# Graph attention on one core: the column of ones written by GpSimd, three one-hots cast together one tile ahead, a third buffer for the turned one-hots

## The chip, the core and the metric

The program runs on one core of a Trainium2 chip. The core has a matrix engine (TensorE, "PE" in the profile, its weight loads "PEld"), a vector engine (VectorE, "DVE"), a scalar engine (ScalarE, "ACT"), a general engine (GpSimd, "POOL", which also issues the indirect DMAs of this kernel) and a DMA-issuing engine (SyncE, "SP"). The metric is the device time of one execution in microseconds. Before the change it is 3703.74 us, the median of 9 runs from 3694.52 to 3710.56 us.

## What is computed

A graph of 3,125 nodes with 256 features and 53,125 edges sorted by destination goes through eight layers, each added to its input: graph attention, a small mixture of experts, three rounds of graph convolution, a routed mixture of experts, and so on. The change lies in the first layer, the attention:

```python
q = (nfeat @ Wq.T).reshape(n, HEADS, HEAD_DIM) / SCALING
k = (nfeat @ Wk.T).reshape(n, HEADS, HEAD_DIM)
v = (nfeat @ Wv.T).reshape(n, HEADS, HEAD_DIM)
attn = jnp.einsum('ehd,ehd->eh', k[src], q[dst]) + attn_bias
a = jnp.exp(attn - m[dst])                    # m: maximum over a node's edges
a = a / segment_sum(a, dst)[dst]
out = segment_sum(v[src] * a[:, :, None], dst).reshape(n, FEAT) @ Wo.T
```

There are 8 heads of 32 features each. For each edge the key and value rows of its source are needed, and the query of its destination; what the edges give is summed by destination.

## The kernel before

**Tiles.** The 3,125 destinations are 25 tiles of 125 (`T`, `P`). Since the edges are sorted by destination, a tile's edges are one window of 18 chunks of 128 edges (`WC`), handled as three parts of 6 chunks (`PC`). Keys and values of all nodes are computed in the beginning and written to `kv_d` in HBM, one row of 512 numbers per node.

**A tile's data.** Each part has a tile `kv` of [128 edges, 6 chunks, 528 columns] float32 (line 1652, seven buffers, so two tiles and a part). Columns 16 to 527 hold the gathered key and value rows, one indirect DMA for each chunk (line 1661), 18 for a destination tile. Column 15 (`KO - 1`) holds ones, so that the sum over the edges also counts them; VectorE writes it after the six gathers are issued (line 1667). Columns 7 to 14 later take the weights of the 8 heads.

`oh` (line 1821, two buffers, bf16) is the one-hot of an edge's destination within the tile, an edge per partition, made by VectorE (line 282, called from `one_hot`). `oht` (line 1811, two buffers, bf16) is the same turned, a destination per partition: SyncE loads the edges' destinations, spread over the partitions (issued by `move`, lines 107 and 108), and VectorE compares them in place (line 1839). `oh_f` (line 1893, two buffers) is a part of `oh` cast to float32 by ScalarE (line 1894).

**The steps of a tile t.** `asked` issues the loads. `one_hot`, `one_hot_turned` and `queries` (lines 1820 to 1840) make the two one-hots and the query in three bf16 pieces (`q_t`). `logits` (line 1842), once for each part, multiplies `oht` by the pieces (TensorE, line 1851, results `qx` in two PSUM buffers), multiplies the keys by that in place (VectorE, line 1854) and sums by head (line 1855). `sums_of` adds the bias (line 1861), takes a scaled exponential (ScalarE, line 1864), sums it by destination (TensorE, line 1867) and copies the sums (ScalarE, line 1869). `weights_of` makes a shift from these (line 1875), brings it to the edges (TensorE, line 1879), subtracts it (lines 1880 and 1882) and takes the exponential into `kv` (ScalarE, line 1884). `weighted` (line 1886) multiplies the values by the weights (VectorE, line 1889, in place), casts the one-hot and accumulates 18 chunks in `acc` (TensorE, line 1896, 36 matmul records a tile). When a part's matmuls have read its `kv` buffer, that buffer is free, and the next six gathers into it can start. `normed`, `normed_turned` and `projected` divide, transpose and project the result and add it to `x`.

**The order of the work.** The loop at line 1927 works on three tiles at once: loads for t + 1, logits and sums of t ("now"), weights and accumulation of t - 1 ("before"), one-hots and queries of t + 1 ("after"):

```python
if now: logits(now, 0)
beside()
if before: weights_of(before); beside(); weighted(before)
beside()
if after: one_hot(after)
if before: normed(before)
if after: one_hot_turned(after); queries(after)
...
if now: logits(now, 1)        # then normed_turned, logits(now, 2), projected, sums_of
```

`beside` is a step of the next layer's experts (`Experts0`, line 793) for pairs of finished tiles, and from tile 5 on there are steps of `Windows` (line 1988). They share all engines with the attention. This is not the order of issue: when the program is built, each engine's instructions are put into one fixed sequence, the earlier in the text the sooner, but an instruction that is planned to be ready may pass one that is not. In the trace the query product of line 1828 for tile t + 1 (at 542.3 us) stands ahead of the accumulation of tile t - 1 (548.9 us), though the text has it behind. On the chip an engine then keeps to its sequence and waits wherever an instruction isn't ready. The time at which a buffer comes free is part of that plan.

On GpSimd a gather also waits until the one five before it has landed (`under_way`, lines 1664 and 1665).

Of the kernel before, what the change touches and what calls it, by code (L numbers as in the profile page):

```python
# [10 lines left out]
F32 = mybir.dt.float32  # L11
F32R = mybir.dt.float32r
I32 = mybir.dt.int32
BF16 = mybir.dt.bfloat16
# [9 lines left out]
P, T = 125, 25  # L24
# [24 lines left out]
WC, PC = 18, 6  # L49
# [21 lines left out]
def gnn_ffn_kernel(ctx: ExitStack, tc: tile.TileContext, a, out: bass.AP):  # L71
    nc = tc.nc
# [32 lines left out]
    def move(queue, to, of):  # L105

        queue.dma_start(to[:SPREAD], of[:SPREAD])
        return queue.dma_start(to[SPREAD:], of[SPREAD:])
# [1518 lines left out]
    def attention(windows, experts):  # L1627
# [9 lines left out]
        KO, VO, AO = 16, 16 + D, 7  # L1637
        WB = T * WC // 5
        with ExitStack() as es:
# [11 lines left out]
            def rows_tile():  # L1651
                return tiles.tile([128, PC, 2 * D + KO], F32, name="kv", bufs=7)
# [3 lines left out]
            def gathered(at):  # L1656


                kv = rows_tile()
                for c in range(PC):  # L1660
                    got = nc.gpsimd.indirect_dma_start(  # L1661
                        out=kv[:, c, KO:], out_offset=None, in_=kv_d,
                        in_offset=bass.IndirectOffsetOnAxis(ap=src_i[:, at + c:at + c + 1], axis=0))
                    if len(under_way) > 4:
                        tc.add_manual_dep(got.ins, under_way[-5].ins.name, data_dep, reason="in turn")
                    under_way.append(got)
                nc.vector.memset(kv[:, :, KO - 1:KO], 1.0)
                return kv


# [1 line left out]
            pool = setup.enter_context(tc.tile_pool(name="att_in", bufs=2, reuse_waits="tile"))  # L1672
# [107 lines left out]
            for i, (t0, n) in enumerate(GROUPS):  # L1780
                both = rows_tile().rearrange("p c w -> p (c w)")
                ln = both[:P, :4 * D].rearrange("p (i d) -> p i d", i=4)
                kv = both[:P, 4 * D:12 * D].rearrange("p (i d) -> p i d", i=4)
# [17 lines left out]
            pool = es.enter_context(tc.tile_pool(name="att_s", bufs=2, reuse_waits="tile"))  # L1801
# [6 lines left out]
            def asked(t):  # L1808
                s = Tile()
                s.t, s.kv = t, begun if t == 0 else []  # L1810
                s.oht = pool.tile([P, WC, 128], BF16, name="oht")
                move(nc.sync, s.oht.rearrange("d c e -> d (c e)"), turned_d[t * WC:(t + 1) * WC, :].rearrange("(o c) e -> o (c e)", o=1)
                     .to_broadcast([P, WC * 128]))
                s.lt = pool.tile([128, 2, P], F32, name="lt_t")
                nc.sync.dma_start(s.lt, lt_d[:, :, t, :].rearrange("k f p -> f k p"))
                s.eb = pool.tile([128, H, WC], F32, name="eb_t")
                nc.sync.dma_start(s.eb, eb_d[:, t])
                return s

            def one_hot(s):  # L1820
                oh = pool.tile([128, WC, HC], BF16, name="oh")
                one_hots(oh, row_h[:, s.t * WC:(s.t + 1) * WC, :], iota_h)
                s.oh = oh[:, :, :P]
# [13 lines left out]
            def one_hot_turned(s):  # L1837
                v = s.oht.rearrange("d c e -> d (c e)")
                nc.vector.tensor_scalar(v, v, pcol[:P], None, ALU.is_equal)
                s.l = pool.tile([128, WC, H], F32, name="l")  # L1840

            def logits(s, p):

                if p == len(s.kv):
                    s.kv.append(gathered(s.t * WC + p * PC))
                kv = s.kv[p]
                for c0 in range(0, PC, 2):
                    ps = psum.tile([128, 2, D], F32, name="qx", bufs=2)
                    for c in range(2):
                        for k in range(3):  # L1850
                            nc.tensor.matmul(ps[:, c, :], s.oht[:, p * PC + c0 + c, :], s.q[:, k, :],  # L1851
                                             start=(k == 0), stop=(k == 2))
                    k_ = kv[:, c0:c0 + 2, KO:VO]
                    nc.vector.tensor_mul(k_, k_, ps)  # L1854
                nc.vector.tensor_reduce(  # L1855
                    s.l[:, p * PC:(p + 1) * PC, :],
                    kv[:, :, KO:VO].rearrange("p c (h d) -> p c h d", h=H), AX.X, ALU.add)
# [13 lines left out]
            def weights_of(s):  # L1871

                m = pool.tile([P, H], BF16, name="m")
                c = 8.0 * math.log(2.0)
                nc.vector.tensor_scalar(m, sums[:, s.t, :].bitcast(I32), c / 2.0 ** 23, -127.0 * c,
                                        ALU.mult, ALU.add)
                ps = psum.tile([128, WC, H], F32, name="sm")
                for c in range(WC):
                    nc.tensor.matmul(ps[:, c, :], s.oht[:, c, :], m, start=True, stop=True)
                nc.vector.tensor_sub(s.l, s.l, ps)  # L1880

                nc.vector.tensor_scalar(s.l, s.l, 20.0, None, ALU.min)
                for p in range(WC // PC):
                    nc.scalar.activation(s.kv[p][:, :, AO:AO + H], s.l[:, p * PC:(p + 1) * PC, :], AF.Exp)

            def weighted(s):
                s.acc = psum.tile([P, 512], F32, name="acc", bufs=1)
                for p, kv in enumerate(s.kv):
                    nc.vector.tensor_mul(  # L1889
                        kv[:, :, KO:VO].rearrange("p c (h d) -> p c h d", h=H),  # L1890
                        kv[:, :, VO:].rearrange("p c (h d) -> p c h d", h=H),
                        kv[:, :, AO:AO + H].unsqueeze(3).to_broadcast([128, PC, H, HD]))
                    of = pool.tile([128, PC, P], F32, name="oh_f")
                    nc.scalar.copy(of, s.oh[:, p * PC:(p + 1) * PC, :])
                    for c in range(PC):
                        nc.tensor.matmul(s.acc[:, :D + H + 1], of[:, c, :], kv[:, c, AO:VO],  # L1896
                                         start=(p == 0 and c == 0), stop=(p == 2 and c == PC - 1))


            def normed(s):  # L1900
                nc.scalar.copy(deg[:, s.t:s.t + 1], s.acc[:, H:H + 1])
                inv = pool.tile([P, H], F32, name="inv")
                nc.vector.tensor_scalar(inv, s.acc[:, 0:H], 1.0e-30, None, ALU.max)
                nc.vector.reciprocal(inv, inv)
                s.ao = pool.tile([P, D], F32, name="ao", bufs=1)
                nc.vector.tensor_mul(s.ao.rearrange("p (h d) -> p h d", h=H),
                                     s.acc[:, H + 1:D + H + 1].rearrange("p (h d) -> p h d", h=H),
                                     inv.unsqueeze(2).to_broadcast([P, H, HD]))

            def normed_turned(s):  # L1910
                ps = psum.tile([128, 2, P], F32, name="sm")
                for k in range(2):
                    nc.tensor.transpose(ps[:, k, :], s.ao[:, k * 128:(k + 1) * 128], ident[:P, :P])
                s.at = pool.tile([128, 2, P], F32, name="at", bufs=1)
                nc.scalar.copy(s.at, ps)

            def projected(s):
                po = psum.tile([P, D], F32, name="sm")
                product(po, [(s.at[:, k, :], wo[:, k, :]) for k in range(2)])
                nc.vector.tensor_add(x[:, s.t, :], x[:, s.t, :], po)  # L1920

            now, before = asked(0), None
            one_hot(now)
            one_hot_turned(now)
            queries(now)
            more = experts()
            for t in range(T + 1):
                def beside():
                    more.step(t - 1)

                after = asked(t + 1) if t + 1 < T else None
                if now:
                    logits(now, 0)
                beside()
                if before:
                    weights_of(before)
                    beside()
                    weighted(before)
                beside()
                if after:  # L1940
                    one_hot(after)
                if before:
                    normed(before)
                if after:
                    one_hot_turned(after)
                    queries(after)
                beside()
                if now:
                    logits(now, 1)
                beside()  # L1950
                if before:
                    normed_turned(before)
                beside()
                if now:
                    logits(now, 2)
                if before:
                    projected(before)
                beside()
                if now:
                    sums_of(now)  # L1960
                beside()
                if t >= Windows.TB:
                    windows.next()
                before, now = now, after
# [568 lines left out]
```

## Time and profile before

| what | value |
|---|---|
| median of 9 runs | 3703.74 us |
| the profiled execution, its own time | 3704.48 us |
| span of its instructions | 3702.3 us |
| busy: PE, DVE, ACT, POOL | 86%, 46%, 28%, 18% of the span |
| attention's gathers (line 1661), first and last issue | 97.7 and 1153.5 us |
| one gather's time on GpSimd, median | 946 ns |
| accumulation, line 1896: matmul time in all | 232.2 us |
| VectorE's one-hot, line 282, in the attention | 1341 ns (median) |
| turned one-hot, line 1839 | 812 ns (median) |
| cast to float32, line 1894 | 819 ns (median) |
| VectorE's column of ones, line 1667 | 63 ns, 75 times |

The page's groups of instructions give line, engine, operation and tiles, then busy time, the mean of one, the idle time of the engine just before them and what ended most of that. The list of waits says which instruction waited for which, with the sum, the number and the longest. In the timeline the first two columns are the start and the time taken; what stands in brackets is the engine's idle time before it and what ended it. The table by stretches gives the busy time of each engine with its instructions, the granted TensorE clock as a share of full speed, the share of time in which the 16 DMA engines were busy, and GB/s. "remote" and "another core or an unknown queue" stand for a semaphore whose raiser the profile can't match; there is no other core here.

### The profile page before, as it was taken

How to read it: one execution, taken by the hardware profiler on the slowest of the kernel's cores; microseconds unless marked ns; L12 is line 12 of the kernel's file. 1: busy time of each engine (PE TensorE's matmuls, PEld its weight loads, DVE VectorE, ACT ScalarE, POOL GpSimd, SP SyncE). 2: the span in 40 equal slices, each digit the busy share in tenths (PEclk: the TensorE clock that was granted, in tenths of full speed). 3: DMA queues.
4: the chain of work that ended last, by engine and by line, in shares of the span. 5: the costliest groups of instructions: out<-in, count | busy, mean ns of one | idle time of the engine just before them, and what ended most of it. 6: DMA issues, size and time to landing. Idle time of an engine off the chain costs nothing.

```text
span 3702.3 us, 44414 instructions
## 1 busy us (share of the span) xinstructions
PE 3183.7 (86%) x16137; PEld 2459.2 (66%) x16137; DVE 1720.0 (46%) x4788; ACT 1027.9 (28%) x2074; POOL 669.2 (18%) x639
## 2 busy tenths in 40 slices
PE   6567777677767888999999789997999999999898
PEld 2345555555546777898988678886875555568766
DVE  6455555555546875342456712214651111254672
ACT  1112222212112454232323222223432323332130
POOL 1543444344441000000002433320000000000000
PEclk9767887878778999999999899998999999999998
DMA  5744444444441467443434466665320000034101
GB/s 167 228 141 121 127 121 128 123 128 127 128 129 48 135 213 198 102 109 102 118 93 108 117 182 183 175 188 128 96 62 17 17 9 9 15 79 104 42 1 36
DMA packets 257582, 402.72 MB, mean 109 GB/s; under 512 B 42704, under 2 KB 202319, under 8 KB 257348
## 3 DMA queue, kind: packets, MB, share of 16 engines
q1 hardware_dynamic: 188465, 241.20, 23.4%
q0 software_dynamic: 54064, 141.25, 14.1%
q10 hardware_dynamic: 14819, 17.27, 1.8%
q8 instruction: 132, 2.16, 0.2%
q14 instruction: 102, 0.84, 0.1%
HBM read 328.87 MB, written 70.70 MB: 108 GB/s over the span
## 4 chain that ended last, share of the span: by engine, by line
PE 71%; DVE 7%; another core or an unknown queue 5%; issue 4%; ACT 2%; DMA 2%; ACTq 0%; SPq 0%; POOL 0%; DVEq 0%; POOLq 0%
PE agg L2236 19%; PE po L266 18%; PE hid_ps L266 14%; PE acc L1896 5%; PE tr L266 4%; PE qx L1851 2%; PE row L266 1%; PE tok L1536 1%; DVE kv L1854 1%; DVE l L1855 1%; PE sm L266 1%; PE tr L2324 1%; PE tr L250 1%; PE pair L266 1%
## 5 line engine op out<-in xcount | busy, mean ns | idle before, releaser
L2236 PE MATMUL agg<-cnt_f,hp 125*128 125x500 f32 (+1 forms) x3500 | 733.7, 369 | 22.3 <-ACT hp L2177 22.3
L2236 PEld LDWEIGHTS agg<-cnt_f,hp 125*128 125x128 f32 x3500 | 635.9, 189 | 103.0 <-ACT hp L2177 23.4
L1661 POOL DMA_INDIRECT kv<-kv_d,src_w x450 | 440.1, 978 | 528.7 <-PE acc L1896 392.4
L2214 ACT CAST cnt_f<-blk 125x500 fp32r<-125x500 bf16 (+1 forms) x435 | 245.5, 566 | 518.5 <-PE agg L2236 495.8
L1851 PE MATMUL qx<-q_t,oht 125*128 125x256 bf16 x1350 | 228.7, 315 | 107.1 <-DVE kv L1854 87.1
L2214 DVE CAST cnt_f<-blk 125x500 fp32r<-125x500 bf16 (+1 forms) x440 | 185.3, 423 | 265.5 <-PE agg L2236 221.5
L1382 DVE SCALAR_TENSOR_TENSOR x<-po,gall,x 125x256 f32<-125x256 f32 x200 | 93.9, 484 | 417.4 <-PE po L266 416.9
L1376 ACT ACTIVATE h<-hid_ps,shift,scale 128x500 f32<-128x500 f32 (+1 forms) x224 | 161.7, 722 | 376.2 <-PE hid_ps L266 375.6
L1851 PEld LDWEIGHTS <-oht 125*128 125x128 bf16 x1350 | 150.4, 113 | 164.8 <-issue 122.3
L1896 PE MATMUL acc<-kv,oh_f 128*125 128x265 f32 x900 | 232.2, 418 | 3.8 <-DVE kv L1889 3.8
L1854 DVE TENSOR_TENSOR kv<-kv,qx 128x512 f32<-128x512 f32 x225 | 150.5, 682 | 170.1 <-remote 114.5
L1896 PEld LDWEIGHTS acc<-kv,oh_f 128*125 128x125 f32 x900 | 182.7, 205 | 42.6 <-DVE kv L1889 5.1
L266 PE MATMUL po<-wslot,h 128*125 128x256 f32 x800 | 203.0, 386 | 0.1
L266 PE MATMUL hid_ps<-h,wslot 128*128 128x500 f32 (+1 forms) x448 | 193.6, 555 | 4.1 <-ACT h L1376 0.6
L266 PEld LDWEIGHTS po<-wslot,h 128*125 128x125 f32 x800 | 145.1, 187 | 75.2 <-ACT h L1376 27.0
L266 PE MATMUL hid_ps<-xe,wslot 128*128 128x256 f32 x832 | 186.9, 382 | 1.8 <-DVE xe L1214 1.8
L266 PE MATMUL hid_ps<-v_rows,wslot 128*128 128x500 f32 (+1 forms) x448 | 186.8, 537 | 0.0
L266 PE MATMUL po<-wslot,hid 128*128 128x256 f32 x832 | 184.5, 378 | 0.0
L1225 ACT ACTIVATE hid<-hid_ps,wslot 128x256 f32<-128x256 f32 x208 | 98.3, 474 | 286.7 <-PE hid_ps L266 277.6
L1072 POOL DMA_INDIRECT xs_d<-r_l,pos x50 | 60.1, 1203 | 643.6 <-DVE r_l L1068 567.6
L266 PEld LDWEIGHTS hid_ps<-xe,wslot 128*128 128x128 f32 x832 | 150.6, 191 | 33.0 <-ACT hid L1225 3.4
L266 PEld LDWEIGHTS po<-wslot,hid 128*128 128x128 f32 x832 | 155.6, 189 | 21.8
(512 smaller groups left out, 4604.9 us busy)
## 6 DMA issues: line engine op xcount, KB each, us to landing
wslot<-in_ex_W SPq DMA_DIRECT2D x52, 1024.0 KB
blk<-an_d SPq DMA_DIRECT2D x60, 546.9 KB
blk<-at_d SPq DMA_DIRECT2D x40, 546.9 KB
blk<-an_d SPq DMA_DIRECT2D x45, 410.2 KB
at_d<-ab SPq DMA_DIRECT2D x25, 683.6 KB
an_d<-an SPq DMA_DIRECT2D x25, 683.6 KB
oht<-turned_d SPq DMA_DIRECT2D x25, 504.0 KB
blk<-at_d SPq DMA_DIRECT2D x30, 410.2 KB
```

The source lines that it names most:

```text
L250: nc.tensor.transpose(ps[:, i * P:(i + 1) * P], src[:, i, k * 128:(k + 1) * 128], ident[:P, :P])
L266: nc.tensor.matmul(ps, l, r, start=(bias is None and i == 0), stop=(i == last))
L1072: st = nc.gpsimd.indirect_dma_start(out=xs_d, in_=l2[:, i, :].bitcast(I32), in_offset=None, out_offset=bass.IndirectOffsetOnAxis(ap=self.p ...
L1225: nc.scalar.activation(hid[:, m, :], ps[:, :BLK], AF.Gelu, bias=c[:, 4 + m:5 + m])
L1376: nc.scalar.activation(dst[:, m, :c], ps[:, :c], AF.Relu, bias=shift[:, l, col:col + 1], scale=scale[:, l, col:col + 1])
L1382: nc.vector.scalar_tensor_tensor(x[:, t0 + i, :], po, gating.all[:, t0 + i, e:e + 1], x[:, t0 + i, :], ALU.mult, ALU.add)
L1661: got = nc.gpsimd.indirect_dma_start(out=kv[:, c, KO:], out_offset=None, in_=kv_d, in_offset=bass.IndirectOffsetOnAxis(ap=src_i[:, at + c: ...
L1851: nc.tensor.matmul(ps[:, c, :], s.oht[:, p * PC + c0 + c, :], s.q[:, k, :], start=(k == 0), stop=(k == 2))
L1854: nc.vector.tensor_mul(k_, k_, ps)
L1896: nc.tensor.matmul(s.acc[:, :D + H + 1], of[:, c, :], kv[:, c, AO:VO], start=(p == 0 and c == 0), stop=(p == 2 and c == PC - 1))
L2214: to(f[:, :n, :], part[0][:, :n, m % MB, :])
L2236: nc.tensor.matmul(ps[f][:, :c], hp[:, m, k, f * 128:(f + 1) * 128], got[:, :c], start=(m == 0 and k == 0), stop=(m == T - 1 and k == 1))
```

## The change

Three edits, all in `attention`. The column of ones is written by GpSimd, ahead of the six gathers of its part instead of by VectorE behind them. The turned one-hot gets three buffers in place of two. The casts to float32 leave `weighted`; a new function `cast` makes all three for the tile "now", in the iteration in which `weighted` works on the tile before it, into three buffers in place of two, so that `weighted` finds them one iteration later.

```diff
                 kv = rows_tile()
+                nc.gpsimd.memset(kv[:, :, KO - 1:KO], 1.0)
                 for c in range(PC):
                     got = nc.gpsimd.indirect_dma_start(
...
                     under_way.append(got)
-                nc.vector.memset(kv[:, :, KO - 1:KO], 1.0)
                 return kv
...
-                s.oht = pool.tile([P, WC, 128], BF16, name="oht")
+                s.oht = pool.tile([P, WC, 128], BF16, name="oht", bufs=3)
...
+            def cast(s):
+                s.oh_f = []
+                for p in range(WC // PC):
+                    s.oh_f.append(pool.tile([128, PC, P], F32, name="oh_f", bufs=3))
+                    nc.scalar.copy(s.oh_f[-1], s.oh[:, p * PC:(p + 1) * PC, :])
+
             def weighted(s):
...
-                    of = pool.tile([128, PC, P], F32, name="oh_f")
-                    nc.scalar.copy(of, s.oh[:, p * PC:(p + 1) * PC, :])
+                    of = s.oh_f[p]
...
                     weights_of(before)
                     beside()
                     weighted(before)
+                if now:
+                    cast(now)
                 beside()
                 if after:
                     one_hot(after)
```

## The prediction, made before the changed kernel was run

> **What bounds the kernel now.** The table by stretches comes first, for the attention's steady part and for two neighbouring tiles within it, cut where a run of gathers begins and where it has landed.
>
> ```profile
> 160.00:1160.00 1000.00, 709.51 (x3888) 528.63 (x3886) 542.50 (x1105) 199.61 (x479) 414.83 (x416) 0.79 0.44 126
> 463.90:489.60 25.70, 16.58 (x85) 12.04 (x85) 11.63 (x30) 3.63 (x7) 17.62 (x18) 0.94 0.65 184
> 489.60:513.80 24.20, 19.10 (x108) 14.58 (x108) 18.46 (x29) 5.72 (x14) 0.01 (x1) 0.64 0.13 33
> 513.80:539.60 25.80, 14.60 (x83) 10.87 (x81) 10.28 (x34) 4.15 (x11) 17.59 (x18) 0.83 0.64 187
> 539.60:552.80 13.20, 12.81 (x64) 9.59 (x65) 9.50 (x11) 4.06 (x13) 0.00 (x0) 0.81 0.17 53
> ```
>
> After the time come PE, PEld, DVE, ACT and POOL busy, then clock, DMA share and GB/s. No engine is full over the 1,000 us. The work alternates: a **burst** of 18 gathers, 25.7 to 25.9 us in each of the 22 full bursts that begin between 169.2 and 1,088.4 us, then a **gap** without gathers, 24.2 us after one tile and 13.2 after the next. Bursts take 22 x 25.8 = 568 us of the 970 between 169.2 and 1,139.2.
>
> The list of waits says what begins a burst, and what VectorE waits for.
>
> ```profile
> POOL kv L1661 <- PE acc L1896: 392.4, 22, 28.0
> ...
> DVE kv L1854 <- remote: 114.5, 26, 11.7
> ...
> DVE oh L282 <- ACT oh_f L1894: 22.7, 18, 2.4
> ...
> DVE kv L1667 <- PE acc L1896: 20.9, 10, 2.6
> ```
>
> A burst begins when the accumulation (line 1896) has read the first `kv` buffer. It ends 25.8 us later because GpSimd issues a gather every 1.25 us and the last lands some 3.8 us after its issue. "Remote" is TensorE itself: by the trace's semaphore events its completions are counted 0.0 us after the recorded end in the gaps, but up to 15 us after it in a burst, from 7 to 11 us into it, and all are let through when the last gather has landed. So most of what needs a TensorE result late in a burst waits for the burst's end; the chain of waits between 140 and 1,200 us has 201.5 us of it, against 164.8 of the accumulation. **The burst's length is paid in full.**
>
> The timeline of one burst's beginning shows all that the change touches.
>
> ```profile
> 507.85 11.28 PE L1896 MATMUL acc<-kv,oh_f 128*125 128x265 f32 x36 [0.37 <-DVE kv L1889]
> ...
> 511.13 0.81 DVE L1839 TENSOR_SCALAR oht<-oht,pcol 125x2304 bf16<-125x2304 bf16 x1
> ...
> 513.55 0.82 ACT L1894 CAST oh_f<-oh 128x750 f32<-128x750 bf16 x1 [7.29 <-PE acc L1896]
> 513.79 0.94 POOL L1661 DMA_INDIRECT kv<-kv_d,src_w  x1 [27.05 <-PE acc L1896]
> 514.40 1.34 DVE L282 TENSOR_TENSOR oh<-iota_a,row_w 128x2268 bf16<-128x2268 bf16 x1 [2.40 <-ACT oh_f L1894]
> 515.04 1.52 POOL L1661 DMA_INDIRECT kv<-kv_d,src_w  x1 [0.30 <-issue]
> ...
> 516.49 0.82 ACT L1894 CAST oh_f<-oh 128x750 f32<-128x750 bf16 x1 [2.11 <-PE acc L1896]
> 516.87 0.95 POOL L1661 DMA_INDIRECT kv<-kv_d,src_w  x1 [0.30 <-issue]
> ...
> 517.56 0.08 DVE L1667 MEMSET kv<- 128x6 f32 x2
> ```
>
> All of VectorE's waits stand beside the accumulation, which keeps TensorE until 519.1. And the one-hot of line 282, which waits for a cast, falls upon the second gather: that takes 1.52 us in place of 0.95.
>
> **The change, part by part.**
>
> *Ones by GpSimd.* It removes 75 VectorE memsets of 63 ns and 20.9 us of waiting, and adds 75 GpSimd memsets ahead of six gathers each, 68 of them in the 23 bursts (22 x 3 + 2). What VectorE gains is hidden: those waits end with the accumulation's parts, and what follows them on VectorE (line 1903, at 519.36) needs its end anyway. Cover gone, it would be worth 20.9. The memset takes over the wait for the buffer that the first gather has now; queued behind it are the gathers, which wait for the same. TensorE must now see a GpSimd semaphore too, set some 40 us earlier. The cost is GpSimd's time, since a gather's wait for the one five back has 6.25 - 3.8 = 2.4 us to spare. The trace has no GpSimd memset among gathers. The nearest row is a memset of one column.
>
> ```profile
> L2524 POOL MEMSET const-float32-1.0<- 128x1 f32 x1 | 0.1, 101 | 0.0
> ```
>
> From below: it is not free, as GpSimd does one thing at a time; a tenth of a us, 68 x 0.10 = 6.8 us. From above: 0.10 and another handover of 0.30 as between two gathers, 68 x 0.40 = 27.2. I take 6.8, because the 0.30 is paid ahead of the next gather already and the compute rows at the program's start follow each other without a pause.
>
> The gathers' lengthening shows a lock between the two engines: over all gathers, what those above 1.05 us take beyond 946 ns is 12.2 us where line 282 runs beside them (22 gathers), and 2.3 us elsewhere. The Trainium skill, "SBUF — State Buffer", section "SBUF: two separate sides", says that VectorE in a two-port mode and GpSimd lock each other out for a whole instruction, which speaks against a memset there: if each burst's first one met line 1839, it would by that rule wait up to 0.81 us, 23 x 0.81 = 18.6 us more. No run here shows a memset in that place, and 1839 mostly ends before the burst.
>
> *Casts a tile ahead.* Three casts of 0.82 us stay three, on an engine busy 200 of 1,000 us. In the trace the casts in one accumulation are the last part of its own tile and two parts of the next; with three buffers they are the three of the next, released by the same matmuls. TensorE has waited for no cast (its waits at line 1896 are for line 1889, 8.9 us), so it gains nothing. What goes is VectorE's 22.7 us: the buffer of `oh` is now free when the sums (line 1867) have read it, ahead of the gap, not inside the next burst. So line 282 can be planned earlier, and with that the gather's lengthening goes: **-12.2 us**. The wait itself lies on the chain with 2.7 us of line 282 and 3.2 of line 1894; I take **-5.9**. What is late next is TensorE's delayed signals, which could swallow the 5.9 (bound: 0); the other bound is the 22.7.
>
> The price: earlier means in the gap, where VectorE is busy 18.46 of 24.2 us. A 1.34 us instruction there costs nothing where VectorE waits for TensorE anyway (495.5 to 496.8 us, behind the sums), and 1.34 us a tile where it delays line 1875. I take 0; dear case below.
>
> *Third turned one-hot.* The load (562 KB in two DMAs, SyncE) now waits for line 1879 of the tile before the one it waits for now, so it runs one tile earlier but again in a gap, where the DMA share is 0.13 to 0.17. Line 1839 has waited for it once, 1.1 us, so directly 0. Cover gone, it is 4.2 us (issued 452.4, landed 456.6). The loads of `lt_t` and `eb_t` behind it on SyncE are not needed sooner. Line 1839 may move like line 282; 0.81 us, again taken at 0.
>
> Sum: -12.2 - 5.9 + 6.8 = -11.3 us. Against the profiled execution's own 3704.48 us (span 3702.3 and 2.2 around it) that is 3693.2; the median is 0.7 lower, so I say **3693 us**, 0.3% faster. About 0.2% (7.4 us) is what a measurement can tell from no change.
>
> **Rivals.**
>
> *GpSimd gives it back (slower).* Place: GpSimd inside each burst. At 0.40 us a memset, and line 282 still meeting some gather, the sum is +27.2: 3731. It decides from 18.1 / 68 = 0.27 us a memset on. For it: GpSimd paces the burst. Against: the 101 ns row. 0.22.
>
> *VectorE's order gets worse (slower).* Lines 282 and 1839 come to stand in front of line 1889 in the gap, 2.15 us a tile: 23 x 2.15 = 49.5, with -12.2 + 6.8 a sum of +44: 3748. For it: they leave a place beside the accumulation, where they are free. Against: at the sums VectorE waits anyway. 0.14.
>
> *Nothing moves.* The plan leaves line 282 where it is or puts it upon another gather, and the other waits were covered: +6.8 at most, 3704 to 3711, about 3707. 0.20.
>
> *One more handover before the signals get late (faster).* The 24.2 us gap is long since logits of the third part are still open when the burst ends (line 1854 at 479.1, 484.7 and 490.0), the 13.2 us gap short since they are not. VectorE is free 3.7 us sooner (2.40 + 1.34). If that saves the handover in every long gap, 11 x 11.0 = 121 us are to be had; half of it and the forecast's sum give 3633. Against: TensorE, not VectorE, is behind in the first 5 us of a burst. 0.14.
>
> **The numbers.** The forecast has 0.30, from 3680 to 3696. Faster is 0.30 + 0.14 = 0.44, same 0.20, slower 0.22 + 0.14 = 0.36. With both signs in play the range reaches towards the handover case on one side (half of its way, 3650) and to the dear memset and most of the order case on the other (3745); some 0.08 and 0.08 stay outside.
>
> **What would show it.** Right: second gathers of 0.95 us, line 282 without a wait and not in a burst's first us, bursts of 25.8 - 0.55 + 0.3 = 25.5 us, gaps unchanged. The memset's price is seen as the distance between the sixth and seventh gather, now 1.25 us: 1.35 by the forecast, 1.65 by the first rival. Wrong: line 1875 or 1889 behind line 282 with longer gaps; bursts longer than 26.5 us; or long gaps near 13 us, and then the gain is far larger than forecast. The planned order is the weak point: I read it from the sequence of before, and a shift of 1.5 us a tile either way is 33 us.

## The result, and the profile after

The changed kernel takes 3737.92 us (median of 10 runs) beside 3704.39 for the kernel before (31 runs): ratio 1.0095, 95% interval 1.0082 to 1.0107. It is slower by 33.5 us where 3693 was forecast, faster by 11. The profiled execution has a span of 3742.2 us, 39.9 more than before.

The same table by stretches as before, for the attention's steady part and for the same two tiles, cut where a run of gathers begins and where it has landed (PE, PEld, DVE, ACT, POOL busy, then clock, DMA share, GB/s):

```profile
160.00:1160.00 1000.00, 700.25 (x3700) 522.39 (x3700) 512.20 (x969) 190.67 (x457) 412.49 (x470) 0.77 0.43 122
477.10:503.40 26.30, 14.25 (x78) 10.85 (x77) 9.52 (x25) 2.48 (x6) 18.27 (x20) 0.86 0.63 179
503.40:527.20 23.80, 18.80 (x104) 14.41 (x104) 18.20 (x31) 6.25 (x15) 0.14 (x2) 0.65 0.13 33
527.20:552.70 25.50, 10.39 (x54) 7.80 (x52) 9.38 (x26) 2.37 (x8) 17.48 (x20) 0.76 0.66 189
552.70:571.50 18.80, 18.21 (x107) 13.81 (x108) 11.78 (x16) 5.84 (x16) 0.11 (x1) 0.87 0.14 38
```

The long gap is nearly as it was (23.8 us beside 24.2), the short one has grown from 13.2 to 18.8. In the burst before it TensorE starts 54 matmuls instead of 83: work that stood inside the burst now stands behind it. Over the 22 full bursts the mean distance from burst to burst went from 44.09 to 45.71 us, and all of it is gap: the bursts are 0.15 us shorter (22 x 0.15 = 3.3 us won), the gaps 1.77 longer (38.9 lost). With 2.1 us before the first burst and 2.1 after the last that is the 39.9. In the changed kernel line 1660 is GpSimd's memset, 1662 the gather, 1895 the product with the values (1889 before), 1901 the accumulation (1896) and 1918 the turning of the result (1913); the other lines named here keep their numbers.

The list of waits, from 140 to 1,200 us:

```profile
POOL kv L1660 <- PE acc L1901: 240.6, 11, 28.0
...
DVE kv L1854 <- remote: 83.2, 18, 12.6
...
ACT g_turned L226 <- remote: 39.2, 5, 12.6
...
DVE oh L282 <- remote: 29.0, 4, 11.6
...
DVE oh L282 <- PE sm L1867: 15.0, 7, 3.3
```

GpSimd's wait for the accumulation now stands at the memset (line 1660), in 11 of the bursts by this list; it waits for VectorE too, and most of the others are put down to that. The one-hot of line 282 waits for no cast any more, as forecast; it waits for the sums (line 1867) and for TensorE's late completions, so it has left the burst's head. Line 226, ScalarE's copy of Experts0's gates, waits 39.2 us for "remote" (five times) where it waited 11.7 us (three times).

The head of a burst in the timeline (start, time taken, idle time before and what ended it), and one memset inside it:

```profile
526.51 0.11 POOL L1660 MEMSET kv<- 128x6 f32 x1 [26.20 <-PE acc L1901]
...
527.17 0.95 POOL L1662 DMA_INDIRECT kv<-kv_d,src_w  x1 [0.55 <-issue]
...
528.43 0.95 POOL L1662 DMA_INDIRECT kv<-kv_d,src_w  x1 [0.30 <-issue]
...
529.20 0.80 DVE L1839 TENSOR_SCALAR oht<-oht,pcol 125x2304 bf16<-125x2304 bf16 x1
...
529.68 1.14 POOL L1662 DMA_INDIRECT kv<-kv_d,src_w  x1 [0.31 <-issue]
...
542.10 0.13 POOL L1660 MEMSET kv<- 128x6 f32 x1
542.41 0.95 POOL L1662 DMA_INDIRECT kv<-kv_d,src_w  x1 [0.18 <-issue]
```

The second gather takes 0.95 us, not 1.52. The memset inside the burst stands in the handover that was paid anyway: 1.25 us from gather to gather, with or without it (medians). The first memset of a burst does cost: a gap of 0.55 us follows it, and the first gather comes 0.77 us after the accumulation's first part instead of 0.27 (medians of 22).

The end of that burst and the gap behind it show where the tile is lost:

```profile
545.60 0.36 ACT L226 COPY g_turned<-tr 4x250 f32<-4x250 f32 x1 [12.60 <-remote]
546.00 2.04 PE L266 MATMUL tr<-lt,wslot 128*128 128x250 f32 x4 [10.64 <-issue]
...
547.83 0.62 PE L1918 MATMUL sm<-ident,ao 125*128 125x125 f32 x2
...
552.64 0.47 ACT L781 ACTIVATE s<-tr,wslot 128x250 f32<-128x250 f32 x1 [6.69 <-remote]
553.01 0.31 ACT L1864 ACTIVATE el<-l 128x144 bf16<-128x144 f32 x1
...
554.99 1.91 PE L266 MATMUL sm<-wo,at 128*125 128x256 f32 x4
...
557.92 1.16 PE L1867 MATMUL sm<-el,oh 128*125 128x8 bf16 x18
...
559.12 1.34 DVE L282 TENSOR_TENSOR oh<-iota_a,row_w 128x2268 bf16<-128x2268 bf16 x1 [1.08 <-PE sm L1867]
...
560.38 0.17 DVE L1875 TENSOR_SCALAR m<-sums 125x8 bf16<-125x8 int32 x1
```

The same steps of the same tile before, where the burst began at 513.79 and landed at 539.6:

```profile
520.28 0.43 PE L1913 MATMUL sm<-ident,ao 125*128 125x125 f32 x2
...
524.01 0.36 ACT L226 COPY g_turned<-tr 4x250 f32<-4x250 f32 x1 [2.54 <-PE tr L770]
...
529.60 0.47 ACT L781 ACTIVATE s<-tr,wslot 128x250 f32<-128x250 f32 x1 [5.23 <-remote]
529.97 0.31 ACT L1864 ACTIVATE el<-l 128x144 bf16<-128x144 f32 x1
...
531.16 2.03 PE L1867 MATMUL sm<-el,oh 128*125 128x8 bf16 x18
```

Line 226 came 10.2 us into the burst and now comes after 18.4; the sums came after 17.4 us, inside the burst, and now after 30.7, behind it; and the one-hot of line 282 holds line 1875 up by its 1.34 us right behind them. I call a tile's sums "inside" when their last matmul ends over 1 us before the last gather has landed. Before, 11 of 22 tiles had them inside, with a mean gap of 13.6 us, the others 23.3; after, it is 5 tiles (14.7) and 17 (21.9).

### The profile page after: what moved, and what is told of

It reads as the page before. It is cut to its first block, busy times and chain, and to the rows that moved or that the text cites. A ratio compares the mean times of both kernels' runs of the same rounds, so it can differ in the third digit from the quotient of the medians.

```text
span 3742.2 us, 44491 instructions
## 1 busy us (share of the span) xinstructions
PE 3212.6 (86%) x16137; PEld 2482.8 (66%) x16137; DVE 1720.0 (46%) x4713; ACT 1029.3 (28%) x2074; POOL 679.9 (18%) x714
## 4 chain that ended last, share of the span: by engine, by line
PE 72%; issue 8%; DVE 7%; another core or an unknown queue 4%; DMA 4%; ACT 2%; POOL 2%; SPq 0%; ACTq 0%; POOLq 0%; DVEq 0%
PE agg L2243 19%; PE po L266 17%; PE hid_ps L266 14%; PE acc L1901 4%; PE tr L266 4%; PE qx L1851 2%; POOL kv L1662 2%; PE row L266 1%; PE sm L266 1%; PE tok L1536 1%; PE tr L250 1%; PE sm L1867 1%; DVE kv L1854 1%; PE tr L2331 1%
## 5 line engine op out<-in xcount | busy, mean ns | idle before, releaser
L266 PE MATMUL tr<-lt,wslot 128*128 128x250 f32 (+1 forms) x312 | 103.7, 462 | 77.5 <-issue 65.1
```

The costliest lines, as they stand in the source:

```text
L266: nc.tensor.matmul(ps, l, r, start=(bias is None and i == 0), stop=(i == last))
```

## The experiments

All ratios are to the kernel before on the same chip. The other columns are read from each run's profile as above: mean distance of the 22 bursts, burst (first issue to last landing, taken as 3.8 us after the last issue), gap, and tiles with their sums inside. The program behind the last burst takes 2,557 to 2,572 us in all of them, so the difference is made in these bursts and gaps.

| run | ratio | distance | burst | gap | inside |
|---|---|---|---|---|---|
| before | 1 | 44.09 | 25.6 | 18.4 | 11 |
| after | 1.0095 | 45.71 | 25.5 | 20.2 | 5 |
| e1 ones alone | 1.0085 | 45.38 | 25.3 | 20.1 | 7 |
| e2 casts alone | 1.0154 | 47.11 | 25.2 | 21.9 | 1 |
| e3 third turned one-hot alone | 0.9949 | 43.49 | 26.0 | 17.5 | 12 |
| e4 casts and third one-hot | 1.0142 | 46.54 | 25.4 | 21.2 | 3 |
| e5 casts, pause late in the burst | 1.0167 | 46.04 | 25.8 | 20.3 | 2 |
| e6 after, pause late in the burst | 1.0128 | 45.44 | 25.9 | 19.5 | 4 |
| e7 before, a rest in the middle | 0.9709 | 39.23 | 27.3 | 11.9 | 20 |
| e8 after, a rest in the middle | 0.9793 | 40.12 | 26.8 | 13.4 | 19 |
| e9 before, memset at the head | 0.9990 | 44.14 | 25.7 | 18.5 | 12 |
| e10 after, pause early | 1.0031 | 44.82 | 26.0 | 18.8 | 6 |
| e11 casts, pause early | 1.0111 | 46.05 | 25.7 | 20.4 | 3 |
| e12 third one-hot and rest | 0.9698 | 39.50 | 27.7 | 11.8 | 20 |
| e13 after, line 282 tied back | 0.9989 | 43.62 | 25.6 | 18.0 | 9 |
| e14 casts, line 282 tied back | 1.0101 | 45.35 | 25.6 | 19.8 | 5 |
| e15 after, sums first | 1.0170 | 46.35 | 25.5 | 20.9 | 7 |
| e16 before, sums first | 1.0055 | 44.67 | 25.7 | 18.9 | 12 |
| e17 after, tied back, and rest | 0.9808 | 40.91 | 26.8 | 14.1 | 19 |
| e18 before, two rests | 0.9719 | 39.42 | 27.7 | 11.7 | 20 |

The theories: A, the memset at the burst's head; B (later L), line 282's place; C, the sums of every second tile behind the burst; D, the pace of the gathers, which decides when TensorE's completions get late; O, the planned order; Q, the tile before's projection ahead of the sums.

**One edit at a time (e1 to e4).** e1 takes only the memset's line from the change's diff, e2 only the casts, e3 only `bufs=3` of `oht`, e4 the casts and `oht` together.

> The kernel before with the column of ones set by GpSimd and nothing else changed. Theory A (the head of the burst): the first of the three memsets of a tile stands between the end of the accumulation and the first gather, and put that distance from 0.27 to 0.77 us in the changed kernel; 22 x 0.50 = 11 us, so 3704 + 11 = 3715, and the distance from the 6th to the 7th gather stays at 1.26 us, so the other two cost nothing. Theory B (the one-hot of line 282 in the gap) and theory C (the sums of every second tile after the burst, so that the gap of 13.2 us becomes 18.8) both take it to be the casts: by them nothing but A's part moves here and the short gap stays at 13.2 us. If the short gap grows here, it is the memsets, or the order planned anew, that does it.

> The kernel before with the casts a tile ahead and nothing else changed. Theory B: line 282 goes into the gap for 1.34 us in every tile, 22 x 1.34 = 29 us, less the 0.57 us a tile that the second gather is shorter (12.5 us): 3704 + 17 = 3721, and both gaps grow alike, by about 1.3 us. Theory C: the sums (line 1867) of every second tile stand behind the burst, the short gap goes from 13.2 to about 18.8 us and the long one stays, 11 x 5.6 = 62 us less 12.5 of shorter gathers and less what earlier chains give: 3725 to 3750. By the prediction's own step, 3704 - 18 = 3686.

> The kernel before with a third buffer of turned one-hots and nothing else changed. By the prediction's step, by theories A, B and C alike, it is worth nothing: 3704 within 8 us, the gaps at 24.2 and 13.2 us. If the short gap grows here, the third buffer moves the order of the work (line 1839 and the logits before the sums), and the casts are not its cause.

> The changed kernel with the ones set by VectorE again: casts a tile ahead and third buffer of turned one-hots, without the GpSimd memsets. Theory A: the first gather comes 0.27 us after the accumulation again, and the time falls by 11 us from 3738 to 3727; the short gap stays at 18.8 us. If the memsets are the whole loss (rival to A, B and C), it falls to 3704 or below.

Measured: 1.0085 (1.0060 to 1.0109), 1.0154 (1.0130 to 1.0178), 0.9949 (0.9931 to 0.9968), 1.0142 (1.0122 to 1.0163). The casts are the dear edit: by the ratio +57 us at 3710, the median is 3773. C has the sign right and the size short (3773, not 3725 to 3750); the forecast's own step, 3686, is on the wrong side. The third buffer, taken at nothing, wins 0.5%. The ones cost 0.85% alone, three times what A gives, and on top of the other two they win 0.5%: the edits don't add. What these slow kernels share is the last column of the table.

From the first full burst to the start of the 23rd run of gathers, TensorE does the same work in all of them. It is busy for 686 of 970 us in the kernel before, 686 of 998 in e1 and 684 of 1,037 in e2, so what these two lose is waiting. In the changed kernel it is 707 of 1,006 us, at a mean granted clock of 0.77 instead of 0.79. So up to 21 of its 36 us are longer busy time and only 14 are waiting. Whether the lower clock costs time or only goes with it no run here shows; e2, with the larger loss, has 0.77 too and no longer busy time.

In e3 line 1839 stands in the first microseconds of the burst in 19 tiles (before, it stood in the gap in all 22); 22 x 0.81 = 17.8 us is near the gain of some 19 us, but other instructions moved as well, so that this is its source is not shown. It wins although line 1839 lengthens gathers there: the time that gathers over 1.05 us take beyond 946 ns rises from 12.3 to 20.6 us. In e2 line 282 goes the other way, from the burst's head (19 tiles) to the gap (22).

**GpSimd pauses, nothing else (e5 to e8).** Memsets of a spare tile, tied between gathers on GpSimd by order alone; TensorE, VectorE and ScalarE keep the order of the kernel they are compared with (VectorE but for at most six of its short memsets, over the first 1,200 us).

```
+ m = nc.gpsimd.memset(rest, 0.0)     # 128x256; 2 of them (e5, e6) or 3 (e7, e8)
+ tc.add_manual_dep(m.ins, last.ins.name, behind, reason="rest")
```

> The kernel with the casts alone, and two GpSimd memsets of a spare tile (128x256) between the second and the third gather of every tile: a brake of about 0.6 us at the place where line 282 held the second gather up in the kernel before. GpSimd's memsets depend on nothing but the gathers, and all other engines keep their order. Theory D (pace): TensorE's completions are let through while GpSimd pauses, so a burst that starts without a pause has them late earlier (from +5.7 to +7.5 us here against +7 to +11 in the kernel before), the sums (line 1867) of 10 of 11 odd tiles slip behind the burst, and the gap is 21 instead of 13.6 us. By it the brake brings the onset back to +7 us or later and the sums of some odd tiles into the burst: each saves some 7 us, so 3773 + 13 - 30 to 70 = 3716 to 3756. Theory O (order): the changed order of the work on TensorE and VectorE does it, the pause costs its length, 3773 + 22 x 0.6 = 3786.

> The changed kernel with the same brake of two GpSimd memsets between the second and third gather of a tile. Theory D: the sums of the odd tiles that stand behind the burst (7 of 11) come back into it, 3738 + 13 less up to 7 x 5.5 = 3712 to 3738. Theory O: 3738 + 13 = 3751, with the sums where they are.

> The kernel before with three GpSimd memsets of a spare tile (128x256, some 0.9 us) ahead of the 7th and of the 13th gather of every tile; the order of TensorE, VectorE and ScalarE is that of the kernel before. If the burst's length is paid in full and nothing else moves (theory O): 22 x 1.6 = 35 us, 3704 + 35 = 3739. Theory D: TensorE's late completions get through in the two rests, so more of the chain stands inside the burst and the gaps shrink by at least what the burst grows: 3704 or less, and if the sums of even tiles come into the burst too, down to 3640.

> The changed kernel with the same two rests of some 0.9 us in every tile. Theory O: 3738 + 35 = 3773. Theory D: the completions get through in the rests, the sums of the odd tiles come into the burst again, and the short gap falls from 20 towards 15 us: 3738 + 35 - 11 x 5 = 3718 or less.

Measured: e5 1.0167 (1.0130 to 1.0204), e6 1.0128 (1.0110 to 1.0147), e7 0.9709 (0.9690 to 0.9727), e8 0.9793 (0.9777 to 0.9810). e5 and e6 missed their place: a burst begins with a tile's second group of gathers, so the memsets came some 17 us into the burst, when the completions had long been late, and can't tell the theories apart. e7 and e8 are the study's largest effect. Of the two rests of a tile one lies ahead of the burst, where it is hidden; the other makes the burst's seventh gather come 2.42 us after the sixth instead of 1.25 in e7 (2.20 in e8). In e7 that lengthens the burst by 1.6 us and shortens the gap by 6.5. Theory O had +35 us; it is -104.

What the rest does is seen in the timeline of e7 (a burst that begins at 482.44; by this kernel's numbering line 1872 is the exponential, 1875 the sums):

```profile
490.21 1.07 POOL L1664 MEMSET rest<- 128x256 f32 x3
...
491.08 0.38 PE L770 MATMUL tr<-ident,g 125*4 125x125 f32 x2
491.50 0.36 ACT L226 COPY g_turned<-tr 4x250 f32<-4x250 f32 x1 [1.43 <-PE tr L770]
491.69 0.95 POOL L1667 DMA_INDIRECT kv<-kv_d,src_w  x1 [0.41 <-PE tr L770]
...
493.06 0.47 ACT L781 ACTIVATE s<-tr,wslot 128x250 f32<-128x250 f32 x1 [1.20 <-PE tr L266]
...
493.42 0.31 ACT L1872 ACTIVATE el<-l 128x144 bf16<-128x144 f32 x1
...
494.53 1.16 PE L1875 MATMUL sm<-el,oh 128*125 128x8 bf16 x18
```

Line 226, which waits 12.60 us for "remote" in the changed kernel, follows its TensorE work at once here. Line 781 (another ScalarE step of Experts0), which waited 5.23 us for "remote" in the kernel before, follows TensorE at once as well. The sums stand 12.1 us into the burst, not 17.4 as before. TensorE's completions come through when GpSimd adds a pause of about 1.2 us to the distance of two gathers, and in most bursts they are late by over 1 us again some 4 to 7 us after it.

**GpSimd's part at the head, and the pause in its place (e9 to e12).** e9 adds only a GpSimd memset of an unused column of `kv` (128x6) ahead of each burst's first gather; e10 and e11 put the pause of e5 ahead of the third gather; e12 is e3 with the rest.

```
e9:        + if c == 0 and at % WC == PC: nc.gpsimd.memset(kv[:, :, 0:1], 0.0)
e10, e11:  + two memsets of rest where c == 2 and at % WC == PC
e12:       + three memsets of rest where c == 0 and at % WC == 2 * PC; oht with bufs=3
```

> The kernel before with one GpSimd memset of 128x6 (an unused column of kv) ahead of the first gather of every burst, and the order of TensorE, VectorE and ScalarE untouched: GpSimd's part of the change without anything that the moved memset of VectorE does to the order. Theory D (pace): the burst begins 0.5 us later against line 282, so the second gather is no longer held up by 0.58 us, TensorE's completions get late at +6 instead of +7 to +9 us, the sums of several odd tiles slip behind the burst: 3704 + 11 + 20 to 30 = 3735 to 3745. Theory O (the new order of the work): only the head's price, 3704 + 11 = 3715, with 11 tiles' sums inside the burst as before.

> The changed kernel with two GpSimd memsets of a spare tile ahead of the third gather of every burst. (In the two runs with a brake so far the memsets came 16.3 us into the burst, since a burst begins with a tile's second group of gathers; here they come at +2.5 us.) Theory D: the first late completion moves from +7 to +9 us or later and the sums of the odd tiles come back into the burst: 3738 + 14 less 7 x 5 to 8 us = 3696 to 3717. Theory O: 3738 + 14 = 3752, with 5 tiles' sums inside.

> The kernel with the casts alone and the same two memsets ahead of the third gather of every burst. Theory D: the first late completion moves from +5.7 to +8 us or later, the sums of most odd tiles come back into the burst: 3773 + 14 less 10 x 7 = 3717, 3710 to 3735. Theory O: 3773 + 14 = 3787, with one tile's sums inside.

> The third buffer of turned one-hots alone, with a rest of three GpSimd memsets of a spare tile ahead of the 7th gather of every burst: the two single edits that were faster than the kernel before, together. If they add, 3704 - 104 - 18 = 3582; if the rest has already brought in the sums that the third buffer brought in, 3596.

Measured: 0.9990 (0.9980 to 0.9999), 1.0031 (1.0017 to 1.0045), 1.0111 (1.0094 to 1.0128), 0.9698 (0.9682 to 0.9714). In e9 neither D's loss nor A's 11 us comes. A's price goes with how the memset waits:

```profile
513.48 0.11 POOL L1664 MEMSET kv<- 128x6 f32 x1 [25.96 <-PE acc L1904]
513.73 0.95 POOL L1667 DMA_INDIRECT kv<-kv_d,src_w  x1
```

Here the gather follows 0.25 us after the memset's start, in the changed kernel 0.66. The memset waits for two semaphores here, TensorE's and VectorE's; in the changed kernel and in e1 for a third, GpSimd's own. In e8 and e10 the change's own memset waits for two, and the gather follows 0.25 us after it again. So the third wait is worth 22 x 0.5 = 11 us of the loss at most.

e11 is the clean case for the pace: the burst grows by 0.46 us, the gap shrinks by 1.52, with the order of the other engines kept but for two short memsets of VectorE. So gathers that start at full pace do make the gaps longer here. It gives back about a quarter of the casts' loss, not all: 3 tiles inside, not 10. In e10 the head's handover fell as well (0.77 to 0.32 us), so its gain is not the pause's alone. In e12 the rest and the third buffer don't add: with the rest, the sums are inside anyway.

**The order (e13 to e16).** e13 and e14 tie line 282 behind the last product of `kv` (line 1895) on VectorE (line 1889 before the change); e15 and e16 call the sums first and tie the turned rows and the projection of the tile before behind them on TensorE.

```
e13, e14:  - one_hot(after)
           + with tc.issue_after(before.last.ins): one_hot(after)
e15, e16:  - normed_turned(before) ... logits(now, 2); projected(before) ... sums_of(now)
           + logits(now, 2) ... sums_of(now)
           + with tc.issue_after(now.sum.ins): normed_turned(before); projected(before)
```

> The changed kernel with the one-hot of line 282 tied behind the last product of kv (line 1895) on VectorE, so that it stands in the head of the burst as in the kernel before; nothing else is tied. Theory L (line 282 in the gap is the cause): the sums of at least 9 tiles come inside the burst again, 3738 - 25 to 35 = 3703 to 3713. Theory Q (the tile before's turned rows and projection stand ahead of the sums on TensorE): the sums stay behind, 3730 to 3745.

> The kernel with the casts alone and line 282 tied in the same way. Theory L: 3773 falls to 3705 to 3720, 9 or more tiles with their sums inside the burst. Theory Q: 3755 to 3780.

> The changed kernel with the sums of a tile called ahead of the turned rows and the projection of the tile before, and these tied behind the sums on TensorE. Theory Q: the sums of an odd tile come when the exponentials (line 1864) are done, some 19 us into the burst instead of 28 to 30, so the short gap falls from 20 to 15 us: 3738 - 11 x 3 to 5 = 3685 to 3705, less what the later projection costs the next tile. Theory L: nothing is won, 3738 or more.

> The control: the same two edits in the kernel before, where the turned rows and the projection come 6 to 9 us into the burst, before the completions are late. By theory Q nothing stands in the way of the sums there, and moving the projection behind them can only cost: 3704 to 3740. If it gains as much as in the changed kernel, the order is better in general, and says nothing on the change.

Measured: 0.9989 (0.9979 to 0.9998), 1.0101 (1.0084 to 1.0118), 1.0170 (1.0153 to 1.0187), 1.0055 (1.0038 to 1.0071). e13 takes back the whole loss with the rest of the change left in, the head's 0.77 us too. But the tie makes a new plan: over the first 1,200 us, 286 of VectorE's 1,310 instructions, 96 of TensorE's 629 (repeats counted once) and 85 of ScalarE's 545 do not stand in the changed kernel's order. And of the 46 us that it wins over the same tiles, 33 are TensorE's busy time (674 us, not 707). Two tiles' lines of its timeline:

```profile
418.74 3.43 DVE L1895 TENSOR_TENSOR kv<-kv 128x1536 f32<-128x1536 f32 x2
422.15 1.34 DVE L282 TENSOR_TENSOR oh<-iota_a,row_w 128x2268 bf16<-128x2268 bf16 x1
...
439.38 1.16 PE L1867 MATMUL sm<-el,oh 128*125 128x8 bf16 x18
...
456.97 5.09 DVE L1895 TENSOR_TENSOR kv<-kv 128x1536 f32<-128x1536 f32 x3
461.98 1.33 DVE L282 TENSOR_TENSOR oh<-iota_a,row_w 128x2268 bf16<-128x2268 bf16 x1
```

Line 282 stands behind the products that release the accumulation, so it runs beside TensorE's work as before and nowhere between the sums and line 1875, and the sums of the burst at 424.1 come after 15.3 us. Theory Q falls: with the sums first they do come early in e16 (6 to 7 us into most odd bursts), and the time is worse, by 0.55%; in e15 by 0.75% against the changed kernel. So "inside" is only a sign that the chain got through the burst; calling the sums first, which moves other work as well, wins nothing. In e14 the same tie gives back a third of the casts' loss only.

**Together, and more (e17, e18).** e17 is e13 with the rest of e12; e18 is the kernel before with rests ahead of the 5th and the 11th gather.

> The changed kernel with line 282 tied behind the last product of kv, and a rest of three GpSimd memsets of a spare tile ahead of the 7th gather of every burst. If the place of line 282 and the late completions are separate causes, they add: 3705 - 104 = 3600, as the kernel before with the rest (3596). If the rest had already taken in what line 282 costs, it stays at 3623, as the changed kernel with the rest.

> The kernel before with two rests of three GpSimd memsets, ahead of the 5th and of the 11th gather of every burst, all other engines in the order of the kernel before. If the completions get late some 7 us after the last pause, two rests hold them off for nearly the whole burst: the burst is longer by 1.2 us than with one rest (26 us in all), and the gaps shrink by more: below 3596, 3560 to 3590. If one rest has given all there is, 3596 + 26 = 3622.

Measured: 0.9808 (0.9791 to 0.9826) and 0.9719 (0.9701 to 0.9737). With the rest, the tie wins nothing over e8. But the change's loss is still there with the rest in both: e8 takes 0.9793 / 0.9709 = 1.0087 times as long as e7, though 19 tiles have their sums inside and the head's memset costs only 0.25 us. Over the same tiles TensorE is busy 675 us in e8 and 658 in e7, at clocks of 0.81 and 0.83. What makes this part stays open, and with it whether the new order and the late completions are one loss or two. A second rest wins nothing over one. The best versions are e7 and e12, some 3% faster than the kernel before.

## Why the prediction was wrong, point by point

**"The burst's length is paid in full": false, and the root of it.** It made a shorter burst a gain. The bursts did get shorter, by 0.15 us where 0.25 was forecast, and the kernel got slower. That the 25.5 us of the table meet the forecast is luck: the forecast began at 25.8, the table's measure at 25.6. e2 has the shortest bursts (25.2) and the longest distances (47.1); e7 has bursts of 27.3 and distances of 39.2. What is paid is burst and gap together. The runs with a pause, in which the other engines keep their order, show that the gap shrinks when TensorE's completions get through in the burst (e7: 6.5 us less gap for 1.6 us more burst). I had named the late completions, and then held the gaps constant.

**Ones by GpSimd, +6.8 us.** 0.10 us a memset was wrong in place more than in size: two of three cost at most 0.01 us, the first of a burst 0.50 (11 us). The Trainium skill, "SBUF — State Buffer", section "SBUF: two separate sides", has VectorE and GpSimd lock each other out for a whole instruction. By the prediction's estimate up to 18.6 us more stood to be lost by that. 74 of the 75 memsets take 0.11 to 0.14 us. One of them meets line 1839 and ends only when that has ended:

```profile
844.58 0.81 DVE L1839 TENSOR_SCALAR oht<-oht,pcol 125x2304 bf16<-125x2304 bf16 x1
844.83 0.61 POOL L1660 MEMSET kv<- 128x6 f32 x1
```

So the trace agrees with the page, but it happened once, for 0.5 us, and not at the head of every burst for 18.6. On VectorE's side I had taken the gain as hidden and the new order as free. e1 loses 0.85%, some 31 us, of which its head, with three waits as in the changed kernel, is 11 us at most. What else it changes is the planned order: three short memsets and their waits are off VectorE, and the sums of four more tiles stand behind the burst. Which instruction does it there was not tried.

**Casts a tile ahead, -12.2 and -5.9 us.** The waits for the cast went, and the second gather is 0.95 us, as said. But line 1839 lengthens a gather now (1.14 us), so gathers over 1.05 us give back 4.6 us, not 12.2. And e11, which puts a pause in the place of the lengthened gather, is faster than e2. The step that failed is the price of line 282 in the gap, "I take 0", and with it "gaps unchanged": the gaps grew by 38.9 us in the changed kernel, and the casts alone, which take line 282 from the burst's head into the gap, cost 57. The dear bound, 22 x 1.34 = 29.5 us, is near the loss of 33.5 by chance. Line 282 stands between the sums and line 1875 in 11 of the 25 tiles, 14.3 us at most; in e2 it is the same 11 tiles and 14.3 us, with the larger loss. The rest of the price goes with the new order as a whole, in which the sums of six more tiles stand behind the burst. e13, which ties line 282 back, ends the loss, but it moves many other instructions with it, so that this line alone makes the loss is not shown; with the casts alone the tie gives back a third. What the rest is stays open.

**Third turned one-hot, 0.** Alone -0.5%. That fits the same account in the other direction, line 1839 leaves the gap, but was not tried by itself.

**The rivals.** "VectorE's order gets worse" (3748, chance 0.14) came nearest, with one of its two lines and in 11 tiles: line 282 in front of line 1875, line 1839 not. Its counter-argument, that VectorE waits at the sums anyway, failed: at 559.12 line 282 starts when the sums are done, and line 1875 comes 1.26 us later. "GpSimd gives it back" was to be seen at the seventh gather, 1.65 us; it is 1.25. "One more handover" (3633, faster, 0.14) is real in size, since e7 wins 104 us, but nothing in this change reaches it. The signs I had listed, line 1875 behind line 282 with longer gaps, are what the profile shows; the planned order was the weak point I named, and I gave it too little weight.

## What to carry to other kernels

Where work alternates between a stretch in which signals are late and a gap in which they are not, ask of an edit what must get through before the signals turn late, not only how long the stretch gets: a shorter stretch was slower here, and a pause of 1.2 us in its middle won 3%. An instruction freed from a wait can be planned to another place and take others with it; tying it back to its old place, beside a long accumulation, took back the whole loss in the changed kernel and a third with the casts alone, so it is worth a try, not a rule. And take single edits apart before judging a bundle: here one of three, alone, was a gain.

## What the runs showed of the hardware

TensorE's completions, counted up to 15 us late while GpSimd issues gathers every 1.25 us, are let through in a pause of GpSimd of 0.9 to 1.2 us (e7, e8, e18), and in part in one of half that (e11, 0.54 us): there 0.46 us of longer burst stand against 1.52 of shorter gap. The Trainium skill, "Perfetto Trace Analysis", section "Tensor Engine Instruction (MATMUL, LD_WEIGHTS)", says that a matmul's recorded end is an estimate, and that its semaphore is raised only when PSUM has acknowledged all bytes and then has to propagate. The traces agree that the recorded end and the count are two things; which of the two steps is late, and what the gathers have to do with it, no run here shows.

A GpSimd memset of 128x6 between two gathers costs at most 0.01 us: the median distance of two gathers, with a handover of 0.30 us in it, is 1.25 us with and without. Ahead of the first gather it costs 0.50 us with three semaphores to wait for and 0.05 with two (median distances of 0.77 and 0.32 us against 0.27).
